# One layer of RWKV attention and a mixture of experts: the receptance product of three blocks by seven half-size products for eight, with PSUM laid out anew

## The chip, the cores and the metric

The kernel runs on one core of a Trainium2 chip. The metric is device time in microseconds (us), lower is better. Before the change it is 368.35 us, the median of four runs (367.27 to 368.84). The profile is of one further execution, recorded by the hardware profiler.

## The reference, cut to what matters

x has 2048 tokens of 512 channels in fp32. The layer norm of x feeds two branches, and both are added to x.

```python
rvk = jnp.einsum('btc,dc->btd', x, W_rvk)
r, v, k = jnp.split(rvk, 3, axis=-1)
y = jax.nn.sigmoid(r) * wkv(time_decay, time_first, k, v)
return jnp.einsum('btc,dc->btd', y, W_out)
...
biased = probs + e_score_correction_bias
_, idx = jax.lax.top_k(biased, TOP_K)
...
g = jnp.einsum('bsh,eih->bsei', x, gate_w)
u = jnp.einsum('bsh,eih->bsei', x, up_w)
act = jax.nn.silu(g) * u
expert_out = jnp.einsum('bsei,ehi->bseh', act, down_w)
out = jnp.einsum('bse,bseh->bsh', w_full[..., :n_routed], expert_out)
out = out + x * jnp.sum(w_full[..., n_routed:], axis=-1, keepdims=True)
...
x = x + _L0_attn_ref(xn, L0_attn_W_rvk, L0_attn_W_out, L0_attn_time_decay, L0_attn_time_first) + _L0_ffn_ref(xn, L0_ffn_classifier_w, L0_ffn_e_score_correction_bias, L0_ffn_gate_w, L0_ffn_up_w, L0_ffn_down_w)
```

There are 12 experts, the best two for each token, and four of the 12 only pass the token on, scaled. wkv keeps a running maximum, a numerator and a denominator for every channel, and divides at each token. r, k and v are each a product of 2048 x 512 by 512 x 512.

## The kernel before

**Tiling.** The tokens are four blocks b of TB = 512, the channels four chunks c of CC = 4 (128 partitions each). A unit is a pair (b, c): there are 16. For each unit the kernel needs k, v and r as 128 x 512 tiles, channels on partitions and tokens along the row. xnT[b] holds the transposed layer norm of a block, wrvk_sb the weights, in the order r, v, k.

**Head.** Layer norm, transposes, the router (softmax, best two, lists of tokens by expert) and the first units' products share the first 65 us. The first two units (LEAD = 2) get their products by `project` (L276), three plain products of four 512-wide matmuls each.

**Products by seven for eight.** From the third unit on, `seven` (L396) computes k and v of a unit together. Halves of the weights and halves of the tokens make two-by-two blocks, so two plain products would be eight half-size products; with sums of weights (wsum, made once) and sums of tokens (`sum_tokens`, L370, four tiles S1 to S4 per block, on DVE) it makes seven, M1 to M7. Each half-size product is two matmuls of 128 x 128 by 128 x 256 (L411). Several add up in one PSUM accumulator and are copied out between: p1 takes M1, M6, M7, M4, and p3 takes M5 and M3, and p2 M2 alone. ScalarE (ACT) copies them to k, v and a tile `more` (L436, L446, L451, L459, L470, L473); VectorE (DVE) later adds p2 to half of k and `more` to v (L421). These adds and the token sums of the next block are put on a list `owed`, which `emit_owed` hands out. r of the unit is a plain product: four 512-wide matmuls (`r_step`, L424) into a PSUM tile pr, which ACT reads with the exponential of the sigmoid (L467).

**The recurrence.** `scan` (L299) works through a unit in stages. DVE: a running maximum (L314), two subtractions (L316, L317). ACT: two exponentials (L319, L320). DVE: two scans (L326, L328) with a product by v between (L327), sums with the exponential of r (L335 to L337), a reciprocal in two halves (L340) and the product yT (L343).

**The experts.** There are 23 tiles (TILES) of 128 tokens. A tile's rows are gathered by POOL (L812), copied by ACT as 16-bit halves (`flip`, L879), transposed by a DMA on SP (L881) and put together by ACT (`unite`, L887, tile xgT). Tile 0 is transposed on PE instead (`turn`, L871, L873). The gate and up products follow (L906 into pg; two mixed tiles in L858), then tanh on ACT (L918) and two DVE operations (L919, L920), the down product (`finish`, L854 into po), a scaling on ACT (L938) and an adding indirect write by POOL (L942). `turn_act` (L928) transposes the activations of mixed tiles on PE. Weights gw and dw come by SP's queue.

**Attention rows.** `attention` (L1015) makes 128 rows of the output with four matmuls (L1043, into pw; the last row tile in two halves, L1031), DVE adds them to x's rows (L1055) or to the rows read back from the output (L1052, L1039). Eight row tiles of blocks 0 and 1 lie within the main loop. Their rows of x are read beforehand on SP (`read_xn`) and written by POOL in an adding DMA (`accumulate`, L1012), which shares POOL's queue with the gathers and the experts' writes.

**PSUM.** Four pools of two banks each (L83 to L86): ps_mm (p1, p3, some pw), ps_gu (pg, some pw and pa), ps_o (po, the other pw), ps_tr (p2, pr, px).

**The order.** Everything runs in the order in which it is written (`manual_schedule`). From about 72 us on the order comes from a table: `plan(at, generator)` enters a step at a time, and the steps are sorted by it (L1089 to L1135). Scan stages are entered every UNIT = 17.4 us (L1093), product steps in groups of four, MoE tiles evenly spread, and the attention rows at the group numbers of the dictionary `after` (L1094). Each engine executes its own instructions strictly in that order. Ahead of the table stand `fill(4)`, `emit` and `turn(0)`, which put the last products of block 0 and the first of block 1.

Of the kernel before, what the change touches and what calls it, by code (L numbers as in the profile page):

```python
# [35 lines left out]
P = 128  # L36
# [27 lines left out]
def layer(ctx: ExitStack, tc: tile.TileContext, x, w_rvk, w_out, decay, first, cls, ebias, gu, down, out):  # L64
# [11 lines left out]
    basep = pool("base", 3)  # L76
    small = pool("small", 2)
    kvp = pool("kv", 5)
    erp = pool("er", 4)
    sump = pool("sums", 1)  # L80
    five = pool("five", 2)
    dram = pool("dram", 1, space=bass.MemoryType.DRAM)
    ps_mm = pool("ps_mm", 2, space=bass.MemoryType.PSUM)  # L83
    ps_gu = pool("ps_gu", 2, space=bass.MemoryType.PSUM)
    ps_o = pool("ps_o", 2, space=bass.MemoryType.PSUM)
    ps_tr = pool("ps_tr", 2, space=bass.MemoryType.PSUM)  # L86
    routing = ExitStack()
    rp = routing.enter_context(tc.tile_pool(name="route", bufs=1))

# [209 lines left out]
    def scan(b, c):  # L299

        n = f"{b}_{c}"
        s = state[c]
        w, cf = wdec[:, c : c + 1], cfac[:, c : c + 1]
        k = kvr[b, c, "k"]
        if c == 0:
            yT[b] = xyp.tile([P, CC, TB], F32, tag="xy", name=f"yT{b}")


        obv = wk1.tile([P, 3, TB + 1], F32, tag="obv", name=f"obv{n}")
        nc.vector.tensor_copy(obv[:, :, 0:1], s[:, 0:3].unsqueeze(2))  # L310
        o, bs, bvs = (obv[:, m, 0:TB] for m in range(3))
        o2, b2, bv = (obv[:, m, 1 : TB + 1] for m in range(3))

        nc.vector.tensor_tensor_scan(o2, w.to_broadcast([P, TB]), k, s[:, 0:1], ALU.add, ALU.max)  # L314
        a2 = wk1.tile([P, TB], F32, tag="a2", name=f"a2{n}")
        nc.vector.scalar_tensor_tensor(a2, o, w, o2, ALU.add, ALU.subtract)  # L316
        nc.vector.tensor_sub(b2, k, o2)  # L317
        yield
        nc.scalar.activation(a2, a2, AF.Exp)  # L319
        nc.scalar.activation(b2, b2, AF.Exp)  # L320
        yield

        v = kvr[b, c, "v"]
        sums = wk1.tile([P, 2, TB], F32, tag="sums", name=f"sums{n}")
        sq, sp = sums[:, 0, :], sums[:, 1, :]
        nc.vector.tensor_tensor_scan(sq, bs, a2, s[:, 3:4], ALU.add, ALU.mult)  # L326
        nc.vector.tensor_mul(bv, b2, v)  # L327
        nc.vector.tensor_tensor_scan(sp, bvs, a2, s[:, 4:5], ALU.add, ALU.mult)  # L328

        er = kvr[b, c, "r"]  # L330
        den, num = sq, a2
        if b + 1 < NTB:
            nc.vector.tensor_copy(s[:, 0:3].unsqueeze(2), obv[:, :, TB : TB + 1])
            nc.vector.tensor_copy(s[:, 3:5].unsqueeze(2), sums[:, :, TB - 1 : TB])
        nc.vector.scalar_tensor_tensor(den, b2, cf, sq, ALU.mult, ALU.add)  # L335
        nc.vector.scalar_tensor_tensor(den, er, 1.0, den, ALU.add, ALU.mult)
        nc.vector.scalar_tensor_tensor(num, bv, cf, sp, ALU.mult, ALU.add)  # L337
        yield
        for hs in (slice(0, HALF), slice(HALF, TB)):
            nc.vector.reciprocal(den[:, hs], den[:, hs])  # L340
            if hs.start == 0:
                yield
        nc.vector.tensor_mul(yT[b][:, c, :], num, den)  # L343
        yield
# [17 lines left out]
    def sum_first_weights():  # L362

        wsum[1] = weights(1, 0)
        nc.vector.tensor_sub(wsum[1], weights(1, 0), weights(2, 0))

    def part(b, k, t):
        return xnT[b][:, 2 * k : 2 * k + 2, t * HALF : (t + 1) * HALF]

# [15 lines left out]
    def factors(b, n):  # L385
        return {
            1: lambda: (part(b, 0, 0), weights(2, 0)),
            2: lambda: (part(b, 1, 0), weights(2, 1)),
            3: lambda: (left[b][4], weights(1, 1)),
            4: lambda: (part(b, 1, 1), wsum[4]),  # L390
            5: lambda: (left[b][1], wsum[1]),
            6: lambda: (left[b][2], wsum[2]),
            7: lambda: (left[b][3], wsum[3]),
        }[n]()

    def seven(b, c):  # L396

# [30 lines left out]
        def next_sums(ns):  # L428
            if c == CC - 1 and b + 1 < NTB:
                for m in ns:  # L430
                    owed.append(lambda m=m: sum_tokens(b + 1, m))

        p1 = bank(ps_mm, "mm", "p1_")
        multiply(p1, 1, True, False)
# [17 lines left out]
        yield  # L452
        p2 = bank(ps_tr, "tr", "p2_")
        multiply(p2, 2, True, True)
        owed.append(lambda: add(k[:, :HALF], p2[:, :HALF]))
        next_sums((1, 2))
        yield
        multiply(p1, 7, False, False)
# [12 lines left out]
        yield  # L471
        multiply(p3, 3, False, True)
        nc.scalar.copy(more[:, :HALF], p3[:, :HALF])  # L473
        owed.append(lambda: add(v, more))
        next_sums((4,))
        yield

    def emit_owed(force=False):
        while owed and (force or not head):
            owed.pop(0)()  # L480

    head = True
    units = [(b, c) for b in range(NTB) for c in range(CC)]
# [6 lines left out]
    def all_products():  # L490
        for name, m in (("k", 2), ("v", 1), ("r", 0)):
            for u in range(LEAD):
                yield from project(*units[u], ((name, m),))
        for u in range(LEAD, len(units)):
            yield from seven(*units[u])
        emit_owed()

    products = all_products()
# [5 lines left out]

    def emit(n):
        for _ in range(n):
            owed.pop(0)()

    manual = ExitStack()
    manual.enter_context(tc.manual_schedule())  # L510
# [355 lines left out]

    def turn(i):

        pt = ps_tr.tile([P, CC, P], F32, tag="tr", name=f"px{i}")
        for c in range(CC):  # L870
            nc.tensor.transpose(pt[:, c, :], st[i]["xg"][:, c * P : (c + 1) * P], ident)  # L871
        xgT = wk1.tile([P, CC, P], F32, tag="xgT", name=f"xgT{i}")
        nc.scalar.copy(xgT, pt)  # L873
        st[i]["xgT"] = xgT
# [18 lines left out]
    def up(i, cs):  # L893

        if 0 in cs:
            st[i]["pg"] = ps_gu.tile([P, 2, INTER], F32, tag="gu", name=f"pg{i}")
        pg = st[i]["pg"]
        xgT, w = st[i]["xgT"], st[i]["w"]
        for c in cs:
# [23 lines left out]
            st[i]["actT"] = act.rearrange("p (c t) -> p c t", c=IC)  # L923

    def turn_act(i):
        pt = ps_gu.tile([P, IC, P], F32, tag="gu", name=f"pa{i}")
        for c in range(IC):
            nc.tensor.transpose(pt[:, c, :], st[i]["act"][:, c * P : (c + 1) * P], ident)  # L928
        actT = wk1.tile([P, IC, P], F32, tag="actT", name=f"actT{i}")
# [85 lines left out]
    def attention(b, js=range(NJ)):  # L1015

        for j in js:
            i = b * NJ + j
            if i < (NTB - 2) * NJ - 2 and j % 2 == 0:
                po = ps_gu.tile([P, C], F32, tag="gu", name=f"pw{i}")  # L1020
            elif i < (NTB - 2) * NJ - 2:
                po = ps_o.tile([P, C], F32, tag="o", name=f"pw{i}")
            elif j >= 2 if i in orows else j % 2 == 1:
                po = ps_mm.tile([P, C], F32, tag="mm", name=f"pw{i}")
            else:
                po = ps_o.tile([P, C], F32, tag="o", name=f"pw{i}")
            if i == NT - 1:
                for h, ph in enumerate((po, ps_tr.tile([P, C // 2], F32, tag="tr", name="pw_last"))):
                    hs = slice(h * C // 2, (h + 1) * C // 2)
                    for c in range(CC):  # L1030
                        nc.tensor.matmul(  # L1031
# [51 lines left out]
    emit(2)  # L1083
    fill(4)
    emit(1)
    head = False
    fill(4)
    turn(0)
    DONE = 11 + 9 + 16 + 2 + 12  # L1089
    STEPS = 2 * 3 * CC + 11 * (len(units) - LEAD)  # L1090


    UNIT = 17.4  # L1093
    after = {10: (0, 0), 11: (0, 1), 16: (0, 2), 17: (0, 3), 30: (1, 0), 31: (1, 1), 38: (1, 2), 39: (1, 3)}  # L1094
    groups = (STEPS - DONE) // CC + len(after)
    total = groups * 3.43 + TILES * 5.2
    table = []

# [5 lines left out]
    for u in range(1, len(units)):  # L1104
        for at in (0, 5, 7.5, 12, 14):
            plan((u - 1) * UNIT + 9 + at, stages[u])
    plan(2, flip, 1)
    plan(3, gather, 3)
    one = total / groups / CC
    for m in range(groups):  # L1110
# [97 lines left out]
```

## Time and profile before

| What | Value |
| --- | --- |
| median of four runs | 368.35 us (367.27 to 368.84) |
| profiled execution, its own time | 366.76 us |
| its span | 365.0 us |
| PE busy | 358.9 us (98%) |
| DVE busy | 298.5 us (82%) |
| ACT busy | 148.4 us (41%) |
| POOL busy | 88.8 us (24%) |
| DMA queue q1, q0 (share of 16 engines) | 55.7%, 24.7% |

The span is the time from the first to the last recorded instruction; the execution's own time also has what lies around it. PE is TensorE's matmuls, PEld its weight loads, which overlap them. A line of the page's groups names the program line, the engine, the operation, the tiles with shapes, the number, the busy time, the mean of one, and the idle time ahead of it with what ended it. A line of a list of waits reads: engine, tile and line that waited, what it waited for, then the sum in us, the number and the longest. A line of a timeline has the start, the length, the engine, the line and the operation; x4 means that four records lie in it. In a table of windows each engine has its busy time with the number of its instructions in brackets, then the granted TensorE clock, the DMA share and GB/s. The granted clock is full throughout this execution.

### The profile page before, as it was taken

To read this page: it belongs to the slowest core of one execution; us is meant where nothing else is said; L and a number is where in the kernel's file an instruction comes from. 1 tells how busy PE (TensorE), PEld (TensorE's weight loads), DVE (VectorE), ACT (ScalarE), POOL (GpSimd) and SP (SyncE) were. 2 spreads that over 40 slices of the span, in tenths; PEclk is the share of its full clock that TensorE was granted. 3 is DMA by queue.
4 is the path that set the end of the run, shared out by engine and by line. 5 is a ranking of instruction groups with operands and counts; after the bars stand their busy time and mean duration, and the time that the engine had idled before them with its cause. 6 is when DMAs were issued, how large, how long until landed. Compare 5 with 4: busy or idle time off the path is not lost. (4 is left out here: it accounts for less than half of the span.)

```text
span 365.0 us, 5058 instructions
## 1 busy us (share of the span) xinstructions
PE 358.9 (98%) x1768; PEld 240.6 (66%) x1768; DVE 298.5 (82%) x508; ACT 148.4 (41%) x267; POOL 88.8 (24%) x118
## 2 busy tenths in 40 slices
PE   8999999999999999999999999999999999999996
PEld 3555478688746676476677777787766787764444
DVE  5979989899988676999597967699969498869961
ACT  2666132344555535155433464435453526332000
POOL 6001100411222124132222222333332114212130
PEclk9999999999999999999999999999999999999999
DMA  8998931876767999969998679969799796914782
GB/s 285 403 381 323 374 117 56 331 241 201 186 186 221 317 297 301 294 107 308 326 334 208 129 207 268 271 174 287 189 271 260 220 244 121 333 23 57 175 138 93
DMA packets 47131, 84.44 MB, mean 231 GB/s; under 512 B 26496, under 2 KB 26880, under 8 KB 43328
## 3 DMA queue, kind: packets, MB, share of 16 engines
q1 hardware_dynamic: 39792, 64.05, 55.7%
q0 software_dynamic: 7312, 20.06, 24.7%
q8 instruction: 14, 0.23, 0.2%
q14 instruction: 13, 0.11, 0.1%
HBM read 63.25 MB, written 19.27 MB: 226 GB/s over the span
## 5 line engine op out<-in xcount | busy, mean ns | idle before, releaser
L906 PEld LDWEIGHTS pg<-xgT,gw 128*128 128x128 f32 x672 | 78.4, 192 | 5.9 <-issue 4.9
L906 PE MATMUL pg<-xgT,gw 128*128 128x128 f32 x672 | 78.8, 275 | 0.3 <-DMA gw<-in_gu_dram 0.3
L942 POOL DMA_INDIRECT out_dram<-yo,to_i x23 | 40.7, 1768 | 143.8 <-ACT yo L938 27.8
L340 DVE RECIPROCAL sums<-sums 128x256 f32<-128x256 f32 x32 | 54.6, 1731 | 0.0
L424 PE MATMUL pr<-xnT,wrvk 128*128 128x512 f32 x112 | 53.9, 594 | 0.0
L1043 PE MATMUL pw<-wout_sb,yT 128*128 128x512 f32 x120 | 53.7, 593 | 0.1
L1043 PEld LDWEIGHTS pw<-wout_sb,yT 128*128 128x128 f32 x120 | 22.5, 190 | 26.9 <-issue 26.8
L854 PE MATMUL po<-dw,act 128*128 128x512 f32 x84 | 39.5, 592 | 0.0
L918 ACT ACTIVATE act<-pg 128x256 f32<-128x256 f32 x23 | 8.9, 385 | 69.1 <-PE pg L906 58.9
L919 DVE SCALAR_TENSOR_TENSOR act<-act,pg 128x256 f32<-128x256 f32 x23 | 9.6, 419 | 33.4 <-ACT act L918 33.3
L812 POOL DMA_INDIRECT xg<-xs,token_i x23 | 24.8, 1079 | 45.1 <-DVE empty L763 25.2
L424 PEld LDWEIGHTS pr<-xnT,wrvk 128*128 128x128 f32 x112 | 20.4, 190 | 15.1 <-issue 13.3
L411 PE MATMUL p<-xnT,wrvk 128*128 128x256 f32 x112 | 29.1, 382 | 0.1
L411 PE MATMUL p<-S,wrvk 128*128 128x256 f32 x112 | 28.9, 380 | 0.0
L411 PE MATMUL p<-S,T 128*128 128x256 f32 x112 | 28.8, 379 | 0.0
L326 DVE TENSOR_TENSOR_SCAN sums<-obv,state,a 128x512 f32<-128x512 f32 x16 | 20.5, 1284 | 9.4 <-ACT obv L320 9.3
L411 PEld LDWEIGHTS p<-S,T 128*128 128x128 f32 x112 | 21.0, 190 | 8.7 <-issue 6.2
L854 PEld LDWEIGHTS po<-dw,act 128*128 128x128 f32 x84 | 16.0, 190 | 16.2 <-issue 14.8
L887 ACT COPY xgT<-xq 128x1024 uint16<-128x1024 uint16 x22 | 25.5, 1160 | 0.0
L411 PEld LDWEIGHTS p<-xnT,wrvk 128*128 128x128 f32 x112 | 20.8, 190 | 6.8 <-issue 2.9
L411 PEld LDWEIGHTS p<-S,wrvk 128*128 128x128 f32 x112 | 21.0, 190 | 4.4 <-issue 1.8
L879 ACT COPY xp<-xg 128x1024 uint16<-128x1024 uint16 x22 | 23.0, 1048 | 0.0
(223 smaller groups left out, 483.3 us busy)
## 6 DMA issues: line engine op xcount, KB each, us to landing
gw<-in_gu_dram SPq DMA_DIRECT2D x25, 1024.0 KB
dw<-in_down_dram SPq DMA_DIRECT2D x25, 512.0 KB
x<-in_x_dram SPq DMA_DIRECT2D x16, 256.0 KB
xs<-x SPq DMA_DIRECT2D x16, 256.0 KB
wrvk<-in_w_rvk_dram SPq DMA_DIRECT2D x3, 1024.0 KB
xrow<-xs SPq DMA_DIRECT2D x8, 256.0 KB
out_dram<-xrow POOLq DMA_DIRECT2D x8, 256.0 KB, 6.3
xrows<-xs SPq DMA_DIRECT2D x8, 256.0 KB
```

The lines of the kernel that those rows point to most:

```text
L326: nc.vector.tensor_tensor_scan(sq, bs, a2, s[:, 3:4], ALU.add, ALU.mult)
L340: nc.vector.reciprocal(den[:, hs], den[:, hs])
L411: nc.tensor.matmul(ps[:, :HALF], w[:, k, cs], a[:, k, :], start=(begin and k == 0), stop=(end and k == 1), skip_group_check=True,)
L424: nc.tensor.matmul(pr, wrvk_sb[0][:, k, cs], xnT[b][:, k, :], start=(k == 0), stop=(k == CC - 1))
L812: nc.gpsimd.indirect_dma_start(out=xg, out_offset=None, in_=xs, in_offset=bass.IndirectOffsetOnAxis(ap=token[:, column(i) : column(i) + 1] ...
L854: nc.tensor.matmul(out_, lhs[:, c, :], rhs[0][:, c, :], start=(c == 0), stop=(c == last))
L879: nc.scalar.copy(xp, st[i]["xg"].bitcast(U16).rearrange("p (c h) -> p h c", h=2))
L887: nc.scalar.copy(xgT.bitcast(U16).rearrange("p c (t h) -> p c t h", h=2), st[i]["xq"].rearrange("p (h c) t -> p c t h", h=2),)
L906: nc.tensor.matmul(pg[:, c // IC, c % IC * P : (c % IC + 1) * P], w[0][:, k, rs], xgT[:, k, :], start=(k == 0), stop=(k == CC - 1),)
L919: nc.vector.scalar_tensor_tensor(act, act, 1.0, pg[:, 0, :], ALU.add, ALU.mult)
L942: nc.gpsimd.indirect_dma_start(out=out, out_offset=bass.IndirectOffsetOnAxis(ap=index, axis=0), in_=yo[ps], in_offset=None, compute_op=ALU ...
L1043: nc.tensor.matmul(po, yT[b][:, c, j * P : (j + 1) * P], wout_sb[:, c, :], start=(c == 0), stop=(c == CC - 1),)
```

## The change

r of blocks 1 to 3 (12 units) is no longer a plain product. The seven products are now also made for r, for two chunks of channels at a time: r of chunks c and c+1 takes the places that k and v have in the other. `sevens(b, c, with_r)` makes the steps of one such set, and `pair(b, c)` runs three sets in a fixed order: A (k, v of chunk c), B (k, v of chunk c+1) and R (r of both), 21 steps of two 256-wide matmuls for a pair of units. Block 0 keeps the old way.

The weights for R's seven products come from four DVE operations (`sum_r_weights`), the first two behind `emit(1)`, the other two behind `turn(0)`. R's results are copied out of PSUM by ACT as those of k and v are, two DVE adds follow for each pair, and the exponential of r becomes an ACT operation of its own, in `scan`, between tiles in SBUF.

Behind the products of block 0 `change_banks` closes three of the PSUM pools and opens others: gu 1 bank, p2 1, p1 2, p3 1, pr 1 (both accumulators of R in its halves); ps_o keeps its 2. The eight middle attention rows all use ps_o and stand at other groups. Owed DVE work falls due two product steps after it was noted. `flip(1)` moves from the table to directly behind `turn(0)`. UNIT becomes 17.05, the pool of r tiles grows from 4 to 6, and the scratch memory for DMA descriptors is 8192 where the default is 16384.

```diff
-    erp = pool("er", 4)
+    erp = pool("er", 6)
...
+    def change_banks():
+        early.close()
+        for name, n in (("gu", 1), ("p2", 1), ("p1", 2), ("p3", 1), ("pr", 1)):
+            banks[name] = pool(f"ps_{name}", n, **psum)
...
         er = kvr[b, c, "r"]
+        if b > 0:
+            nc.scalar.activation(er, er, AF.Exp, scale=-1.0)
...
+    def sum_r_weights(first):
+        if first:
+            for n in (2, 3, 4):
+                rsum[n] = sump.tile([P, 2, 2, P], F32, tag=f"R{n}", name=f"R{n}")
+            rsum[1] = r_weights(0, 1)
+            nc.vector.tensor_sub(rsum[3], r_weights(1, 1), r_weights(0, 1))
+            nc.vector.tensor_sub(rsum[1], r_weights(0, 1), r_weights(0, 0))
+        else:
+            nc.vector.tensor_add(rsum[2], rsum[3], r_weights(0, 0))
+            nc.vector.tensor_sub(rsum[4], r_weights(1, 0), rsum[2])
...
+    def sevens(b, c, with_r):
...
+        def at(m):
+            which = {2: "p2", 3: "p3", 5: "p3"}.get(m, "p1")
+            if with_r and which != "p2":
+                ps.setdefault("pr", None)
+                if ps["pr"] is None:
+                    ps["pr"] = bank("pr", f"pr{n}")
+                h = which == "p3"
+                return ps["pr"][:, h * HALF : (h + 1) * HALF]
...
+        def m2():
+            src = multiply(2)
+            owe(lambda: nc.vector.tensor_add(t["k"][:, :HALF], t["k"][:, :HALF], src))
...
+        def m3():
+            src = multiply(3)
+            nc.scalar.copy(t["more"][:, :HALF], src)
+            owe(lambda: nc.vector.tensor_add(t["v"], t["v"], t["more"]))
...
+    def pair(b, c):
+        A, _ = sevens(b, c, False)
+        B, next_sums = sevens(b, c + 1, False)
+        R, _ = sevens(b, c, True)
+        order = "A1 A5 R1 A6 A2 R5 A7 A3 R6 A4 B1 R2 B5 B6 R7 B3 B7 R3 B2 B4 R4".split()
+        done = set()
+        for name in order:
+            while owed and owed[0][0] <= clock[0]:
+                owed.pop(0)[1]()
+            {"A": A, "B": B, "R": R}[name[0]][int(name[1])]()
...
+            clock[0] += 1
+            yield
+
+    def owe(work):
+        owed.append((clock[0] + 2, work))
...
-        for u in range(LEAD, len(units)):
+        for u in range(LEAD, CC):
             yield from seven(*units[u])
+        change_banks()
+        for b in range(1, NTB):
+            for c in range(0, CC, 2):
+                yield from pair(b, c)
...
-        pt = ps_tr.tile([P, CC, P], F32, tag="tr", name=f"px{i}")
+        pt = bank("gu", f"px{i}", (CC, P))
...
-            st[i]["pg"] = ps_gu.tile([P, 2, INTER], F32, tag="gu", name=f"pg{i}")
+            st[i]["pg"] = bank("gu", f"pg{i}", (2, INTER))
...
-        pt = ps_gu.tile([P, IC, P], F32, tag="gu", name=f"pa{i}")
+        pt = ps_o.tile([P, IC, P], F32, tag="o", name=f"pa{i}")
...
-            if i < (NTB - 2) * NJ - 2 and j % 2 == 0:
-                po = ps_gu.tile([P, C], F32, tag="gu", name=f"pw{i}")
-            elif i < (NTB - 2) * NJ - 2:
-                po = ps_o.tile([P, C], F32, tag="o", name=f"pw{i}")
-            elif j >= 2 if i in orows else j % 2 == 1:
-                po = ps_mm.tile([P, C], F32, tag="mm", name=f"pw{i}")
+            if i >= (NTB - 2) * NJ - 2 and (j >= 2 if i in orows else j % 2 == 1):
+                po = bank("p1", f"pw{i}")
             else:
                 po = ps_o.tile([P, C], F32, tag="o", name=f"pw{i}")
...
     emit(1)
+    sum_r_weights(True)
     head = False
     fill(4)
     turn(0)
+    flip(1)
+    sum_r_weights(False)
...
-    UNIT = 17.4
-    after = {10: (0, 0), 11: (0, 1), 16: (0, 2), 17: (0, 3), 30: (1, 0), 31: (1, 1), 38: (1, 2), 39: (1, 3)}
+    UNIT = 17.05
+    after = {10: (0, 0), 12: (0, 1), 16: (0, 2), 18: (0, 3), 28: (1, 0), 30: (1, 1), 37: (1, 2), 38: (1, 3)}
...
-    plan(2, flip, 1)
...
-    nc = bacc.Bacc("TRN2", target_bir_lowering=False, num_devices=1)
+    nc = bacc.Bacc("TRN2", target_bir_lowering=False, num_devices=1, dynamic_dma_scratch_size=8192)
```

## The prediction, made before the changed kernel ran

> **What bounds the kernel now.** I read the page first, for the share of each engine, then what PE waited for, then the chain of waits, and then timelines of the places that the change touches. All times are us of the one profiled execution: its span is 365.0 and its own time 366.76, so 1.76 lie around the span. Part 1 of the page:
>
> ```profile
> PE 358.9 (98%) x1768; PEld 240.6 (66%) x1768; DVE 298.5 (82%) x508; ACT 148.4 (41%) x267; POOL 88.8 (24%) x118
> ```
>
> What PE waited for, with the sum, the number and the longest wait:
>
> ```profile
> PE warm L513 <- DVE ones L136: 1.1, 1, 1.1
> PE pt L244 <- ACT x L233: 0.5, 2, 0.3
> PE pt L244 <- DVE x L231: 0.5, 1, 0.5
> PE pg L906 <- DMA gw<-in_gu_dram: 0.3, 1, 0.3
> ```
>
> The chain that ended last, whose last pieces are:
>
> ```profile
> 344.94 13.11 PE pw L1043 x30
> 358.06 1.73 PE pw L1031 x8
> 359.78 1.74 PE pw_last L1031 x8
> 361.52 0.02 issue
> 361.55 0.42 DVE orows L1039
> ```
>
> PE is busy nearly from end to end, its four waits sum to 2.4, and it carries the end. So a matmul taken from PE is worth its full time as long as PE finds its operands ready afterwards. The granted clock is full in all 40 slices of part 2, so rows of one stage hold in another. DVE (82%) is the next engine, and how it stands is read by stage. The table of windows (PE, PEld, DVE, ACT, POOL busy in 143 to 175) and DVE's list of waits say:
>
> ```profile
> 143.00:175.00 32.00, 31.74 (x162) 18.69 (x161) 29.81 (x42) 14.13 (x24) 10.11 (x8) 1.00 0.94 258
> ```
>
> ```profile
> DVE act L919 <- ACT act L918: 33.3, 14, 4.7
> DVE sums L326 <- ACT obv L320: 9.3, 9, 2.0
> ```
>
> In that stage DVE is busy 29.81 of 32, but over the run it waits 33.3 for MoE activations, up to 4.7 at once. It is a second bound in places, with pauses in which it catches up.
>
> **What the change takes from PE.** One timeline, the start of block 1, gives the prices (start, duration, engine, line, operation):
>
> ```profile
> 66.76 1.03 PE L411 MATMUL p<-S,wrvk 128*128 128x256 f32 x4
> 67.62 1.03 PE L411 MATMUL p<-xnT,wrvk 128*128 128x256 f32 x4
> 68.26 0.68 DVE L377 TENSOR_TENSOR S<-xnT 128x512 f32<-128x512 f32 x1
> 68.48 1.88 PE L424 MATMUL pr<-xnT,wrvk 128*128 128x512 f32 x4
> ...
> 70.20 1.03 PE L411 MATMUL p<-S,T 128*128 128x256 f32 x4
> ...
> 72.85 0.62 ACT L320 ACTIVATE obv<-obv 128x512 f32<-128x512 f32 x1
> ...
> 73.50 1.28 DVE L326 TENSOR_TENSOR_SCAN sums<-obv,state,a 128x512 f32<-128x512 f32 x1 [2.02 <-ACT obv L320]
> 73.62 1.06 ACT L879 COPY xp<-xg 128x1024 uint16<-128x1024 uint16 x1
> ```
>
> Durations of matmuls overlap, so I count from start to start. Each fp32 matmul makes two records. The four narrow records from 67.62 to 68.48 are one product of two 256-wide matmuls: 0.86. The four wide records from 68.48 to 70.20 are two 512-wide matmuls: 1.72. Two units' r took eight wide matmuls, 8 x 0.86 = 6.88; as seven products they take 7 x 0.86 = 6.02. That saves 0.86 a pair. The finer row starts, 429 ns a wide record and 215.5 a narrow one, make it 16 x 0.429 - 28 x 0.2155 = 0.83, and for six pairs **-5.0**.
>
> The Trainium skill, "TensorE: Matmul & The Clock Gate", part "Back-to-back issue gap", speaks against this: in streams of weight loads and matmuls it gives about 81 ns at 128 columns and 131 at 512, so a narrower matmul costs more per column. Put between these, about 98 at 256 columns is my estimate, and 28 narrow records would cost 2.7 where 16 wide ones cost 2.1, some 0.6 a pair slower, +3.9 in all. The trace does not agree: 215.5 is half of 429 within 0.3%.
>
> One small stall goes too: in the old order M4 of a unit and M1 of the next follow at once in the buffers of one pool, and once (115.87) PE started 0.25 late there. In the new order every use of an accumulator stands at least two steps (1.72) behind the one before: **-0.25**. The wait of 0.3 for gw (0.42 from start to start) I leave as it is.
>
> **What it adds on DVE and ACT.** DVE gets, per pair, one 256-wide add (0.41, as L421 of k) and one 512-wide add (0.68, as L421 of v): 6 x 1.09 = 6.5, and once four weight sums of 0.69: 2.8; 9.3 in all, under the 33.3 + 9.3 of its waits. ACT gets per pair six 256-wide copies (0.37, as L446) and two exps from SBUF (0.63, as L319) for two from PSUM (0.60, L467): 2.3, 14 over the run, on an engine busy 41%. Neither is a cost by itself; what counts is where an instruction that waits holds up others behind it.
>
> Head of block 1 (67 to 110). The pair begins A1 A5, while the old unit began M1, r, r, M6, M5. A5 needs the first token sum S1, which DVE ends at 68.26 + 0.68 = 68.94 and which nothing in the change makes earlier; A5 would start at 68.48. Stall **+0.5**. Flip(1) now stands directly behind turn(0): its ACT copy (1.06, L879) and its transposing DMA on SP go ahead of scan (1,0)'s two exps. The DMA comes earlier and holds up nothing I can find on SP; the copy puts the scan from 73.50 to about 75.0. The weight sums (until about 74.2 on DVE) hide in that wait, which was 2.0 before. From here DVE is 1.5 late; the v add, now ahead of the second reciprocal, and the r adds make it 2.2 late at unit (1,1) and 3.4 at unit (1,2). DVE itself keeps nobody waiting, but the exps of a scan (L319, L320) wait for DVE's subtraction, and behind them on ACT stand the copies that free PSUM and the copy xgT (L887) that the next gate products need. At unit (1,1) the exps ended at 87.5 before; 2.2 later, with the activation (0.39) and the copy of B6's product (0.37), gives 90.5, some 0.4 to 0.5 after B7 wants its accumulator: **+0.45**. At unit (1,2) xgT of tile 3 ended at 103.99, 1.79 before its products; 3.4 of lateness leaves **+1.5**, PE standing about where it stood (0.8 gained, 0.95 lost). Head together +2.45, by the rows between 0.5 (all but the first covered) and 4.
>
> Middle. The idle stretches of DVE (4.2 at 117.5, 3.1 at 140.7, 4.0 at 174) return the lateness. The PSUM tiles that became single are covered: between the last write of one use and the first of the next, PE has, by the listing of the changed kernel at these prices, at least 5.2 of other work for gu, 8.8 for p2, 4.4 for ps_o, against an ACT or DVE release that took about 1.4 behind PE for a gate tile, up to 2.7. The moved attention rows issue their xrow reads on SP and their adding writes on POOL at other groups; POOL's gather of tile 15 had some 2.4 of margin and keeps about that. The smaller DMA scratch I cost at nothing, since few descriptors are in flight at a time. **+0.3**, between 0 and 3: the upper end is one lateness like 3.4 in 143 to 175, where DVE had only 2.2 free and gets 1.1 more.
>
> R's two accumulators lie in one bank; R5 waits for ACT's copy of R1. The copy starts 0.41 behind the product and takes 0.37, ended 0.78 after it, while the next R step comes two steps (1.72) later: nothing, if ACT is free. The Trainium skill, "PSUM — Partial Sum Buffer", section on bank collisions, says to guard PSUM by bank and quadrant, not by address; by it this wait is due although the halves do not overlap, and it is counted in the slower rival below.
>
> Tail. The last rows of attention wait for DVE's last scan, which ended at 347.05 against PE's 347.5. That chain gets one v add shorter but starts behind the later r add and behind a PE that ends its MoE tile sooner; by the rows DVE is done 25.4 to 25.9 behind the last gate tile, PE ready at 25.3: **+0.2**, at most 0.8.
>
> **Sum.** -5.0 - 0.25 + 2.45 + 0.3 + 0.2 = -2.3: a span of 362.7 and 364.5 for the profiled kind of execution. The profiled time of before lies 1.6 under the median of its four runs (368.35), so I subtract from the median: 368.35 - 2.3 = 366.05, said as **366.1**. A measurement of this kernel can tell about 0.3%, 1.1.
>
> **Rivals.**
> *The full gain.* DVE and ACT have pauses enough, and the lateness of the head never reaches PE, apart from S1. For it: PE's list names no wait for DVE or ACT behind 45 us. Against: the copies behind exps on ACT had 0.7 to 1.8 to spare, and my lateness is more. -5.25 + 0.5 = -4.75: 363.6. Chance 0.24.
> *The gain is eaten, no change.* The same waits as in my sum, but the head at its upper 4 and the middle at 1: -5.25 + 4 + 1 + 0.3 = 0: 368.4. Chance 0.12.
> *Slower: ACT's queue hands DVE's lateness to PE.* It decides at a lateness of some 2 at a scan's first exps: then the copies behind them come after PE wants the bank pr, p1 or the tile xgT. Each such unit costs the lateness less the slack, 3.4 - 1.8 = 1.6 as at unit (1,2). If DVE does not recover (it has 1.1 more to do per pair, and 2.2 free in 143 to 175), five of the eleven later units at 1.6 make 8: -5.25 + 8 = +2.8: 371. For it: 29.81 of 32. Against: the 33.3 that DVE waited, mostly where a gate tile sets the pace, and that a stalled PE gives DVE time. Chance 0.14, with 0.02 of it for narrow matmuls dearer than the trace has them.
> That the change does not do what it says is excluded for PE's part: the listing of the changed kernel has 84 narrow r matmuls where 48 wide ones were.
> The forecast itself has 0.50. So faster by over 0.3%: 0.50 + 0.24 = 0.74, less 0.02 for its own upper edge: 0.72; within 0.3%: 0.13; slower: 0.15. The range goes from the full gain with the first stall hidden too (363.1) to a third of the slower rival's surplus: 369.3.
>
> **What would show it.** The r products at 215 to 216 ns a record and PE busy near 354; a wait of p3 for S1 of about 0.5 near 68.5; a wait of PE at pg of tile 3 near 106, or of p1 near 90, released by ACT; DVE's wait for L320 at its scan near 75; no PE wait for ACT or DVE between 120 and 320. Wrong it would be if PE's list shows no wait in the head (then about 363.6), or waits for ACT in most units (then 368 and more).

## The result, and the profile after

The changed kernel takes 366.30 us (median of 52 runs), the kernel before 367.45 (78 runs, now that there are more). The ratio is 0.9969, 95% interval 0.9958 to 0.9980: 1.15 us faster, where 2.3 were forecast. The forecast of 366.1 lies only 0.2 from the measured time, and that is in part luck: it was counted down from 368.35, the median of the first four runs of the kernel before, which is 0.90 above the median of all 78. Some executions of these kernels show a mean granted clock of 0.995 or less and take some 2 us longer than the others (four of the six of e8 below, whose other two took 362.29 and 362.78), so that where medians are close the gaps in the traces decide. The profiled execution of the changed kernel has a span of 363.8 for 365.0, and a time of its own of 365.62 for 366.76. Part 1 of the page of the changed kernel:

```profile
PE 354.9 (98%) x1840; PEld 254.0 (70%) x1840; DVE 306.1 (84%) x524; ACT 157.8 (43%) x303; POOL 89.5 (25%) x118
```

PE is busy for 4.0 less, DVE for 7.6 more and ACT for 9.4 more. (The prediction's 5.0 on PE is counted from start to start, and its 9.3 on DVE and 14 on ACT are sums of durations, while in the profile neighbouring instructions overlap a little, as the exponentials and copies from 88.61 on below do.) What PE waited for in the changed kernel:

```profile
PE pg L1011 <- ACT xgT L1040: 1.2, 1, 1.2
PE warm L666 <- DVE ones L148: 1.1, 1, 1.1
PE pt L256 <- DVE x L243: 0.6, 1, 0.6
PE pt L256 <- ACT x L245: 0.5, 2, 0.3
PE p L555 <- DVE S L408: 0.4, 1, 0.4
PE pw L1192 <- DVE xrows L1204: 0.4, 1, 0.4
PE p L555 <- ACT v L578: 0.3, 1, 0.3
PE pg L1059 <- DMA gw<-in_gu_dram: 0.3, 1, 0.3
PE pw L1192 <- DVE xrow L1204: 0.3, 1, 0.3
```

Before, nothing on this list came from DVE or ACT after the head. Now there are five such waits, and each can be dated. I call a **gap** what lies between the starts of two neighbouring matmul records beyond the spacing of their form (112 ns at 128 columns, 215.5 at 256, 429 at 512); a gap is somewhat more than the wait in the list. A gap is named by a time shortly before it begins: the record that comes late starts about the gap and another 0.4 to 0.7 later (A5 at 69.25, tile 3 at 107.56). Gaps of over 0.15 behind 45 us, in us:

| place | before | changed | released by |
| --- | --- | --- | --- |
| 68.2, A5 | - | 0.60 | DVE's token sum S1 |
| 89.5, B7 | - | 0.50 | ACT's copy of B6's product |
| 105.7, gate products of expert tile 3 | - | 1.39 | ACT's copy xgT |
| 115.9, M1 behind M4 | 0.25 | - | |
| gw of an expert tile | 0.42 at 173 | 0.47 at 118.5 | DMA |
| 194.5, attention row tile 3 | - | 0.44 | DVE's addition of row tile 2 |
| 250.8, gate products of tile 16 | - | 0.22 | ACT's copy xgT |
| 343, the If | 0.31 | 0.31 | |
| 345.1, row tile 12 | - | 0.52 | DVE's addition of row tile 8 |

All excess over the spacings behind 45 us sums to 2.3 before and 6.0 in the changed kernel: +3.6 against the 5.0 taken from PE, or -1.4. The spans differ by 1.2; the rest lies in the first 45 us. The two largest places, on ACT (start, duration, engine, line, operation):

```profile
84.45 0.38 ACT L583 COPY more<-p 128x256 f32<-128x256 f32 x1
88.61 0.63 ACT L331 ACTIVATE a<-a 128x512 f32<-128x512 f32 x1 [3.78 <-DVE a L328]
89.21 0.63 ACT L332 ACTIVATE obv<-obv 128x512 f32<-128x512 f32 x1
89.75 0.36 ACT L1071 ACTIVATE act<-pg 128x256 f32<-128x256 f32 x1
90.01 0.36 ACT L578 COPY v<-p 128x256 f32<-128x256 f32 x1
...
102.93 0.37 ACT L574 COPY r<-pr 128x256 f32<-128x256 f32 x1 [0.49 <-PE pr L555]
105.23 0.63 ACT L331 ACTIVATE a<-a 128x512 f32<-128x512 f32 x1 [1.93 <-DVE a L328]
105.83 0.63 ACT L332 ACTIVATE obv<-obv 128x512 f32<-128x512 f32 x1
106.37 1.14 ACT L1040 COPY xgT<-xq 128x1024 uint16<-128x1024 uint16 x1
```

ACT sat idle for 3.78 and for 1.93 in front of an exponential that waited for DVE, with copies queued behind it that TensorE needed: the copy of B6's product could have run at about 88.4, 1.06 behind the start of that product (87.33) as in the kernel before, and xgT at 103.30, when ACT came free.

The chain that ended last, followed back from the end, is PE for the last 20 us in the kernel before and breaks off there. In the changed kernel it goes on, and its shares of the span are:

```profile
PE 53%; DVE 22%; DMA 4%; ACT 3%; issue 2%; SPq 1%; DVEq 0%; ACTq 0%
```

DVE is on the path for a fifth of the span, while PE is as busy as before in per cent. Since the chain of before breaks off, the two cannot be set side by side; but in e11 below, where the gaps of the loop are gone, it reads PE 86%, DVE 8%. So a few short waits were enough to lead that much of the chain over DVE.

One correction of names: where the prediction and the expectations speak of the scans of units (1,0), (1,1) and (1,2) near 74, 89 and 105 us, these are the scans of (0,0), (0,1) and (0,2), which run while the products of block 1 are made.

### The profile page after: what moved, and what is told of

It is laid out like the page before. It is cut to its first block, busy times and chain, and to the rows that moved or that the text cites. A ratio compares the mean times of both kernels' runs of the same rounds, so it can differ in the third digit from the quotient of the medians.

```text
span 363.8 us, 5277 instructions
## 1 busy us (share of the span) xinstructions
PE 354.9 (98%) x1840; PEld 254.0 (70%) x1840; DVE 306.1 (84%) x524; ACT 157.8 (43%) x303; POOL 89.5 (25%) x118
## 4 chain that ended last, share of the span: by engine, by line
PE 53%; DVE 22%; DMA 4%; ACT 3%; issue 2%; SPq 1%; DVEq 0%; ACTq 0%
PE pg L1059 16%; PE p L555 13%; PE pw L1192 8%; PE po L1007 6%; PE pr L555 6%; DVE sums L354 5%; DMA gw<-in_gu_dram 4%; DVE obv L326 2%; DVE sums L340 1%; DVE sums L338 1%; DVE yT L357 1%; PE po L1011 1%; DVE tok L878 1%; PE pg L1011 1%; DVE sums L350 1%
## 5 line engine op out<-in xcount | busy, mean ns | idle before, releaser
L1095 POOL DMA_INDIRECT out_dram<-yo,to_i x23 | 42.3, 1838 | 140.2 <-DMA out_dram<-yo,to_i 25.7
L1192 PE MATMUL pw<-wout_sb,yT 128*128 128x512 f32 x120 | 54.5, 595 | 0.8 <-DVE xrows L1204 0.4
L338 DVE TENSOR_TENSOR_SCAN sums<-obv,state,a 128x512 f32<-128x512 f32 x16 | 20.5, 1282 | 7.1 <-ACT obv L332 6.8
L555 PE MATMUL p<-S,T 128*128 128x256 f32 x96 | 25.0, 382 | 0.3 <-ACT v L578 0.3
L555 PE MATMUL p<-S,wrvk 128*128 128x256 f32 x96 | 24.7, 380 | 0.4 <-DVE S L408 0.4
L555 PE MATMUL p<-xnT,wrvk 128*128 128x256 f32 x96 | 24.7, 379 | 0.0
L555 PEld LDWEIGHTS p<-S,T 128*128 128x128 f32 x96 | 17.9, 190 | 6.8 <-issue 2.4
L340 DVE TENSOR_TENSOR_SCAN sums<-obv,state,a 128x512 f32<-128x512 f32 x16 | 20.6, 1284 | 0.6
L555 PEld LDWEIGHTS p<-S,wrvk 128*128 128x128 f32 x96 | 17.7, 190 | 4.2 <-issue 1.2
L326 DVE TENSOR_TENSOR_SCAN obv<-wdec,state,k 128x512 f32<-128x512 f32 x16 | 20.5, 1279 | 0.0
L555 PEld LDWEIGHTS p<-xnT,wrvk 128*128 128x128 f32 x96 | 17.8, 190 | 3.4 <-issue 1.2
```

The source lines that it names most:

```text
L555: nc.tensor.matmul(dst, rows_(k), a[:, k, :], start=(first and k == 0), stop=(k == 1), skip_group_check=True,)
L1095: nc.gpsimd.indirect_dma_start(out=out, out_offset=bass.IndirectOffsetOnAxis(ap=index, axis=0), in_=yo[ps], in_offset=None, compute_op=ALU ...
L1192: nc.tensor.matmul(po, yT[b][:, c, j * P : (j + 1) * P], wout_sb[:, c, :], start=(c == 0), stop=(c == CC - 1),)
```

## The experiments

My theory: PE saves its full 5.0, and the separate gaps give 3.6 of it back, each through an engine that executes in order and stands in front of a wait for DVE. The rivals: the narrow products save less than 5.0; DVE is a bound all along; the gaps share one slack, so that mending one moves it to the next.

### e1: the first reader of S1 one step later

```diff
+        if (b, c) == (1, 0):
+            order[1:3] = "R1", "A5"
```

> The changed kernel with one swap in the first pair alone: A1 R1 A5 for A1 A5 R1, so that the first step that reads the token sum S1 comes one step (0.86 us) later. The trace of the changed kernel shows TensorE 0.60 us late at that place (A5 behind DVE's S1, L408). Theory A (S1's end on DVE, 69.1, is the cause, and what TensorE loses there is lost for good): that gap disappears, and the time falls by 0.6 us, from 0.9969 of the kernel before to about 0.9953. Rival B (the gap is paid anyway, because DVE and ACT set the pace of the head, and the two later gaps at 89.5 and 105.7 us follow DVE, not TensorE): the gap disappears, the two later gaps grow by as much together, and the time stays (0.9969). I hold B for likelier: the chain DVE subtraction, exponential, copy of the tile for the gate products does not depend on S1's reader.

Measured: 365.33, ratio 0.9939 (0.9910 to 0.9967); the span is 363.0 for 363.8. The gap at 68.2 is gone, those at 89 and 105 are 0.50 and 1.39 as they were, only 0.7 earlier. **A holds, and B, which I had held for likelier, falls.** The reason shows on ACT in this run:

```profile
71.94 0.59 ACT L1028 COPY xgT<-px 128x512 f32<-128x512 f32 x1
72.42 1.05 ACT L1034 COPY xp<-xg 128x1024 uint16<-128x1024 uint16 x1
73.37 0.63 ACT L331 ACTIVATE a<-a 128x512 f32<-128x512 f32 x1
```

The exponential starts at 73.37, in the changed kernel at 74.06. DVE's scan starts from it and the one after it; on ACT both stand behind the copy of px (line L1028 here), and px comes from PE, behind A5. So what PE lost at A5, DVE lost as well. (The verdict rests on the gaps and the spans; the interval of the times reaches to within 0.0002 of B's value.)

### e2: flip(1) where it was

```diff
     turn(0)
-    flip(1)
...
+    plan(2, flip, 1)
     plan(3, gather, 3)
```

> The changed kernel with flip(1) back in the table at 2, that is behind the two exponentials of unit (1,0)'s predecessor scan on ACT, as in the kernel before. In the changed kernel its copy (1.05 us) stands ahead of these exponentials, and DVE's scan at 75.24 waited 0.95 us for them. Theory A (this order is one source of the lateness that the gaps at 89.5 (0.50) and 105.7 us (1.39) show): the scan starts at about 74.3, all that follows on DVE comes 0.95 earlier, the gap at 89.5 is gone and that at 105.7 becomes about 0.9; time 0.95 us less, 0.9943 of the kernel before. Rival B (the added DVE operations alone make the lateness, the flip is hidden): both gaps stay, no change (0.9969). Rival C: the flip's transposing DMA, now later, makes TensorE wait for the tile at 83.7 us, and the time grows.

Measured: 365.20, 0.9938 (0.9909 to 0.9967), span 362.9. The gap at 89.5 is gone, the one at 105.7 is 0.79 for 1.39 (forecast about 0.9), and a new one of 0.26 stands at 83.0, at the gate products of tile 1, whose tile is now late (C, in small); the wait for gw near 118 is 0.71 for 0.47. A holds: the early flip was a source of the lateness, and it was worth only 0.26 to tile 1.

### e3: no additions of r on DVE

```diff
-            owe(lambda: nc.vector.tensor_add(t["v"], t["v"], t["more"]))
+            if not with_r:
+                owe(lambda: nc.vector.tensor_add(t["v"], t["v"], t["more"]))
```

(and the same for the 256-wide addition)

> The changed kernel without the twelve DVE adds of r (256 and 512 wide, one of each for every pair); r of blocks 1 to 3 therefore lacks one of its seven products in one half and the sum of two in the other, everything else is computed. DVE has 6.5 us less to do. Theory A (DVE's lateness reaches TensorE only through ACT's queue in a few places): ahead of the exponentials of the scan at 105.2 stand 0.41 and 0.69 us of these adds, so the gap at 105.7 falls from 1.39 to about 0.3, the tail gap at 345.1 (0.52) shrinks to about 0, the gap at 68.2 (0.60) and that at 89.5 (0.50) stay; 1.4 to 1.9 us less in all, 0.992 to 0.993 of the kernel before. Rival B (DVE is a bound all along the loop): 4 us or more less, 0.986. Rival C (DVE's adds are hidden): no change, 0.9969.

Measured: 364.44, 0.9912 (0.9879 to 0.9945). The gap at 105.7 is 0.45, that at 250.8 is gone, those at 68, 89 and 194 stay. Taking 6.5 us from DVE saves 1.2 by the spans (362.6 for 363.8) and 2.1 by the ratios, not 4: **DVE is no bound all along (B falls), nor are its additions free (C falls)**. One part of A fails: the tail gap is 0.51, as before. It does not hang on these additions.

### e4: two moves in ACT's order

```diff
+    EARLY = {3: 30.9}
...
-        if i + 1 < n:
+        if i + 1 < n and i + 1 not in EARLY:
             unite(i + 1)
...
+            if (u, at) == (1, 5):
+                at = 5.65
             plan((u - 1) * UNIT + 9 + at, stages[u])
+    for i, at in EARLY.items():
+        plan(at, unite, i)
```

> The changed kernel with two moves in ACT's order and nothing else: the exponentials of unit (1,1)'s scan stand behind the activation of tile 1 and the copy of B6's product (instead of ahead of both), and the copy that makes the tile for the gate products of expert tile 3 stands ahead of the exponentials of the next scan. Theory A (the two gaps at 89.5 and 105.7 us, 0.50 and 1.39, come from ACT waiting for DVE with ready copies queued behind it): both gaps disappear, DVE is not slower by it, and 1.9 us are saved: 0.9917 of the kernel before. Rival B (ACT or DVE is simply late by then, whatever the order): the gaps move to the next place where TensorE needs DVE's or ACT's result, and 0.5 us or less are saved (0.9955 and above).

Measured: 363.68, 0.9900 (0.9849 to 0.9950). Both gaps are gone, no new one came, and the excess behind 45 us is 1.9 less. What PE waited for, past the head:

```profile
PE p L555 <- DVE S L408: 0.4, 1, 0.4
PE pw L1194 <- DVE xrows L1206: 0.4, 1, 0.4
PE pw L1194 <- DVE xrow L1206: 0.3, 1, 0.3
PE pg L1059 <- DMA gw<-in_gu_dram: 0.3, 1, 0.3
```

DVE's subtraction ahead of the exponentials at 89 came no earlier than in the changed kernel (18.57 behind the start of A5 in both runs: 69.25 to 87.82, and here 71.35 to 89.92); the copies only no longer stood behind it. A holds.

### c1 and e5: the control, and r as a plain product in the new layout

> The changed kernel itself once more, beside the others on the same chip. Expected as before: 0.9969 of the kernel before, gaps of TensorE at 68.2, 89.5, 105.7, 194.5, 250.8 and 345.1 us.

Measured: 366.10, 0.9964 (0.9943 to 0.9986), span 364.1, with the same gaps at the same places (excess behind 45 us 5.8).

```diff
-        if b > 0:
-            nc.scalar.activation(er, er, AF.Exp, scale=-1.0)
...
-        R, _ = sevens(b, c, True)
...
+                nc.tensor.matmul(
+                    wide["ps"],
+                    wrvk_sb[0][:, k, u * P : (u + 1) * P],
+                    xnT[b][:, k, :],
...
+                    nc.scalar.activation(kvr[b, u, "r"], wide["ps"], AF.Exp, scale=-1.0)
...
+        last = r_of(c + 1, 3), r_of(c + 1, 2)
+        R = dict(zip((1, 5, 6, 2, 7, 3), [r_of(c, k) for k in range(CC)] + [r_of(c + 1, k) for k in range(2)]))
+        R[4] = lambda: [work() for work in reversed(last)]
...
-    sum_r_weights(True)
...
-    sum_r_weights(False)
```

(r of chunk c stands in the steps R1, R5, R6 and R2, r of chunk c + 1 in R7, R3 and twice in R4.)

> The changed kernel with r of blocks 1 to 3 as a plain product again: the eight 512-wide matmuls of a pair stand in the seven places of R's steps, each r whole in the bank pr and read by ACT with the exponential straight from PSUM; R's weight sums and adds are gone. The order of everything else, the PSUM layout, flip(1), the attention rows and UNIT are those of the changed kernel. TensorE has 5.0 us more to do, DVE 9.3 less. Theory A (the seven products are worth their full 5.0 on TensorE, the adds cost 1.4 of it at 105.7 and 250.8, and the new layout and order cost about 2 by themselves): some 3.5 us more than the changed kernel, 1.005 to 1.008 of the kernel before, with the gaps at 68.2 and 194.5 still there, that at 105.7 about 0.3. Rival B (narrow products are worth less than 5.0, and the changed kernel's small gain is mainly that): at most 1.5 us more than the changed kernel, 1.001 or below. Rival C (new layout and order cost nothing): 1.000.

Measured: 368.15, 1.0014 (0.9993 to 1.0036), 2.05 above the control where I expected 3.5. What PE waited for in this kernel, past the head:

```profile
PE p L553 <- ACT k L572: 0.5, 1, 0.5
PE p L553 <- ACT v L576: 0.4, 1, 0.4
PE pw L1211 <- DVE xrows L1223: 0.4, 1, 0.4
```

The first line is A5 again (gap 0.62): ACT's copy of k and DVE's S1 ended 0.15 apart there, and A5 started 0.15 behind S1's end (69.33 and 69.48), as in the changed kernel (69.11 and 69.25). The second is B7 (0.57) and the third the tail (0.57).

The excess behind 45 us is 3.3 here, 2.3 before and 5.8 in the control. So the layout, the order and the flip cost 1.0 by themselves (A said about 2, C nothing; the interval of the times alone would allow no change), and the seven products for r bring 2.5 of gaps with their 5.0: 5.0 - 2.5 = 2.5, and the spans of the two differ by 2.3 (366.4 and 364.1). Rival B read the small distance of the times as narrow products being worth less. Its bound of 1.5 is passed, and the traces say no as well: the work is 5.0 less, and the distance is small because the gaps at 105.7, 118, 194 and 250 are not there with r as a plain product. They do not all hang on r's additions: e3, without these, still has 0.45 at 105.7, 0.35 at 118 and 0.44 at 194. What I had mis-sized is that 2.5, which I put at 1.4; that the gap at 194.5 would stay here and 105.7 keep 0.3 was wrong too. On the other hand the gaps at 68, at 89 and in the tail are here without the seven products for r: they belong to the new layout, order and flip.

### e8, e7 and e11: mending all gaps, and the tail

e8 is e1 and e4 together, with tile 16 in EARLY at 167.3, and:

```diff
-            plan(CC * (m + 1) * one + 1, group)
+            plan(CC * (m + 1) * one + (0.8 if m == 16 else 1), group)
...
+            if i in (NT - 4, NT - 3):
+                po = bank("gu" if i == NT - 4 else "p2", f"pw{i}")
-            if i >= (NTB - 2) * NJ - 2 and (j >= 2 if i in orows else j % 2 == 1):
+            elif i >= (NTB - 2) * NJ - 2 and (j >= 2 if i in orows else j % 2 == 1):
```

> The changed kernel with every gap that its trace shows mended by a move in the order: A1 R1 A5 in the first pair (0.60 at 68.2); the exponentials of unit (1,1) behind the copy of B6's product (0.50 at 89.5); the tile copies of expert tiles 3 and 16 ahead of the exponentials beside them (1.39 at 105.7, 0.32 at 250.8); the DVE addition of attention row tile 2 two tenths earlier in the table, ahead of the next scan's first operations (0.54 at 194.5); the attention row tiles 12 and 13 in the banks gu and p2, which nobody uses by then, for those of ps_o (0.52 at 345.1). Theory A (these gaps are separate, each one a wait in an engine's queue, and nothing else holds TensorE): they add up, 3.8 us less than the changed kernel, 0.986 to 0.988 of the kernel before. Rival B (they share one slack, of DVE): with the first two mended the rest moves elsewhere, and about 2 are saved (0.991). For the tail apart: if the gap at 345 stays with the new banks, it is DVE's last yT and not the bank.

Measured: 364.41, 0.9887 (0.9856 to 0.9919). Every gap of the loop of over 0.15 is gone, that of gw too, but the gap of the tail is 1.30. In this profiled execution TensorE's granted clock was 0.81 between 9 and 18 us, so its span (363.2) says nothing; its gaps do. The wait, and the instructions around it:

```profile
PE pw L1198 <- DVEq L1307: 1.1, 1, 1.1
```

```profile
343.50 0.69 DVE L357 TENSOR_TENSOR yT<-a,sums 128x512 f32<-128x512 f32 x1
344.11 1.40 DVE L1210 SCALAR_TENSOR_TENSOR xrows<-xrows,zw,pw 128x512 f32<-128x512 f32 x2
345.14 3.49 POOL L1169 DMA_DIRECT2D out_dram<-xrows  x4 [7.22 <-DVE xrows L1210]
345.71 3.67 PE L1198 MATMUL pw<-wout_sb,yT 128*128 128x512 f32 x8 [1.13 <-DVEq L1307]
```

Row tile 12 now waits for no addition, but for DVE's queue at the If (L1307), which DVE reaches behind both additions. Two runs tell that apart from mere lateness. The first, e7, has the two bank lines of e8's edit and nothing else:

> The changed kernel with attention row tiles 12 and 13 in the banks gu and p2 for those of ps_o, and nothing else. In the run with all gaps mended the gap near 345 did not go but grew to 1.30, put down to DVE's queue at the If (line 1297 in the changed kernel). Theory A (a PE instruction behind the If that needs a result DVE wrote ahead of it, here the last yT, starts only when DVE has passed the If, that is after both additions of rows 8 and 9; in the old bank the first of them released it 0.7 sooner): the gap grows from 0.52 to about 1.2. Rival B (it grew there only because TensorE had gained time on DVE): it is at most 0.5 here.

Measured (one execution, 366.49): with this edit alone the gap at 345 is 1.23 for 0.52, again released by DVE's queue at the If. So B falls, and the new banks were the wrong cure. The reason that A gives is not shown, though. In e7 row tile 12 started with DVE's first operation behind the If:

```profile
347.22 1.96 PE L1194 MATMUL pw<-wout_sb,yT 128*128 128x512 f32 x4 [1.07 <-DVEq L1299]
347.23 1.41 DVE L1206 SCALAR_TENSOR_TENSOR xrows<-xrows,zw,pw 128x512 f32<-128x512 f32 x2 [0.21 <-DVEq L1299]
```

In the changed kernel the same row tile, behind the same If, needs a result that DVE wrote ahead of the If as well, the addition of row tile 8, and it started 0.7 before DVE's first operation behind the If:

```profile
346.34 6.25 PE L1192 MATMUL pw<-wout_sb,yT 128*128 128x512 f32 x14 [0.35 <-DVE xrows L1204]
347.06 1.41 DVE L1204 SCALAR_TENSOR_TENSOR xrows<-xrows,zw,pw 128x512 f32<-128x512 f32 x2 [0.21 <-DVEq L1297]
```

So a result from ahead of the If does not by itself wait for the If. Why the new banks put the wait there stays open.

The second, e11, is e8 without the two bank lines:

> The run with all gaps mended, but with attention row tiles 12 and 13 in the banks of the changed kernel again. Theory A of the tail (the new banks made it wait for both of DVE's additions): the gap near 345 falls from 1.30 to about 0.6, and the time is 0.7 below that run. Rival B (TensorE only waits for DVE's chain, whatever the bank): the gap stays at 1.3 and the time as well. Against the kernel before I expect 0.987.

Measured: **362.44, 0.9865 (0.9838 to 0.9891)**, the fastest kernel here, 3.7 below the control. Its waits of PE, complete:

```profile
PE warm L668 <- DVE ones L148: 1.1, 1, 1.1
PE pt L256 <- DVE x L243: 1.1, 1, 1.1
PE pt L256 <- ACT x L245: 0.5, 2, 0.3
PE pw L1196 <- DVE xrows L1208: 0.4, 1, 0.4
```

The tail gap is 0.52 again although PE has gained its time on DVE, so it was the banks that made it 1.30. (The times do not show that 0.7: 362.44 here, beside the 362.29 and 362.78 of e8 named with the result.) The excess behind 45 us is 2.3, as in the kernel before: the 5.0 of PE's work is now all gain (367.1 - 362.4 = 4.7). The gaps were separate, and rival "one slack" falls.

### e12: more work behind the last products

```diff
-    after = {10: (0, 0), 12: (0, 1), 16: (0, 2), 18: (0, 3), 28: (1, 0), 30: (1, 1), 37: (1, 2), 38: (1, 3)}
+    after = {10: (0, 0), 12: (0, 1), 16: (0, 2), 18: (0, 3), 28: (1, 0), 36: (1, 1), 37: (1, 2), 38: (1, 3)}
```

(on top of e11)

> The kernel of e11_no_tail_edit with attention row tile 5 (block 1, second) at group 36 instead of 30, behind the last products. TensorE then has 3.44 us more work between the last product and the If, and DVE's last scan, which follows these products, starts 3.44 earlier against it; DVE gets one addition of 0.74 more in that stretch. Theory A (the tail gap is DVE's last scan, 25 us long without a pause, against the work that TensorE has left): the gap near 345 goes, 0.5 us less than e11. Rival B (the scan before it already keeps DVE busy, so that an earlier product starts nothing earlier): the gap grows by the addition's 0.7. Rival C: the two banks of ps_o make row 5 wait for DVE's addition, a new gap ahead of 340.

Measured: 371.59, 1.0106 (1.0066 to 1.0146). Rival C, and dearer than I thought: two waits of about 3 us, the first ending at 323.97, the second at 352.46.

```profile
PE po L1009 <- DVE xrow L1208: 3.2, 1, 3.2
PE pw L1196 <- DVE xrows L1208: 3.0, 1, 3.0
```

```profile
319.86 1.28 DVE L340 TENSOR_TENSOR_SCAN sums<-obv,state,a 128x512 f32<-128x512 f32 x1
...
323.17 0.74 DVE L1208 SCALAR_TENSOR_TENSOR xrow<-xrow,zw,pw 128x512 f32<-128x512 f32 x1
```

The addition that frees row 5's bank for the next down product stands behind a scan on DVE. The tail's 0.5 stays open: no run removed it, and A could not be read here behind C's waits.

Whether the smaller scratch for DMA descriptors costs anything was not tried apart: with the default size the larger tiles of the changed kernel do not fit into SBUF (one pool of 17.0 KB per partition, 15.1 left). No wait in the traces points to it.

## Why the prediction was right, point by point

- **PE, -5.0: right.** The listing has the 84 narrow matmuls for 48 wide ones, their records stand 215.5 apart, and e5 against the control gives 2.3 + 2.5 = 4.8 by spans and gaps. (215.5 is half of 429 within 0.5%, not the 0.3% of the prediction.) The figures of the Trainium skill, "TensorE: Matmul & The Clock Gate", section "Back-to-back issue gap", by which narrow matmuls would be dearer for each column, are not borne out by these fp32 products.
- **The 0.25 of M4 and M1: right**, it is gone. The wait for gw was neither gained nor lost, it moved from 173 to 118.5.
- **Head, +2.45: right, term by term.** A5 0.60 for 0.5, B7 0.50 for 0.45, tile 3 1.39 for 1.5; together 2.49. The named cause of each was tested: S1 (e1), the flip and the additions (e2, e3), ACT's order (e4). What I had wrong afterwards, in e1's expectation, is that DVE's chain is independent of PE there: it starts from px.
- **Middle, +0.3: the first mis-sized term, some 0.8.** All excess between 120 and 320 rose by some 0.8, apart from gw, and the sign "no PE wait for ACT or DVE between 120 and 320" failed. Row tile 3 waits 0.44 at 194.5, since DVE's addition of row tile 2 is entered at 111.44 (the table's own time), just behind a scan's first operations at 111.30, and tile 16's products 0.22 at 250.8 for xgT, again behind a pair of exponentials; each has another 0.1 beside it. Moving these two entries took both gaps away (e8, e11). Each is a near tie in the table that the working looked for only in the head. The cover of the single PSUM banks held: neither p2 nor pr shows a wait, and p3 only that for S1. R's two accumulators share the bank pr, which the Trainium skill ("PSUM — Partial Sum Buffer", section "PSUM bank collisions raise a hardware error") says to guard by bank and quadrant, not by address; no wait of PE for pr is in the list. The worry about 143 to 175 was unfounded: DVE was busy for 27.2 of 32 there, PE for all.
- **Tail, +0.2: the second mis-sized term, 0.52.** The working put it down to the later addition of r, as e3's expectation did, and that was wrong: without r's additions the gap is 0.51 (e3), with r as a plain product 0.57 (e5). The wait is for DVE's addition of row tile 8, which DVE makes behind the last yT; it comes with the new layout and order, and which part of these brings it stays open.
- The sum was -2.3. With the measured terms it is -5.0 - 0.25 + 2.5 + 0.8 + 0.5, some -1.4, and -1.2 by the profiled spans. The forecast's sign, its mechanism and its largest terms were right; its size was double, by the middle and the tail. That the time itself came so near is luck in the part named with the result: the base was 0.90 too high.
- The rivals: the full gain did not come by itself, but e11 shows that it was there to be had. The slower one, lateness handed on by ACT's queue, is the mechanism of three gaps here (89.5, 105.7, 250.8), in three units rather than five or more.

## What to carry to other kernels

When work is moved from the bound engine to one that has slack on average, look at each in-order queue for an instruction that waits for the second engine, and at what stands behind it that the first needs: ACT stood idle for 1.9 us with a ready copy behind an exponential, and two moves by a hair in the table (e4, 1.9 us of gaps) were worth more than the whole change (1.15). Price these places singly, all along the loop and not only where the change starts: near ties in a timetable are where they arise. And a step that ends a wait by a new buffer helps only if the buffer was the last thing to come; here, at an If, it lengthened the wait by 0.7.

## What the runs showed of the hardware that I had not expected

In the tail, a matmul behind the If was released by DVE's passing of the If when it had a bank of its own, and started 0.7 us later than with the bank that DVE's first addition freed (gaps 1.23 and 0.52). Whether that is the chip's doing or comes from how the program's waits are laid at the If, no run here tells.

In e12 the 3.2 us pause was followed by a spell of TensorE at half rate. In the table of windows the granted clock is the column behind POOL's:

```profile
319.00:324.00 5.00, 1.80 (x8) 0.86 (x6) 4.85 (x8) 0.00 (x0) 0.00 (x0) 1.00 0.00 0
324.00:329.00 5.00, 5.00 (x8) 2.17 (x9) 4.96 (x5) 0.69 (x1) 1.57 (x1) 0.66 0.00 0
329.00:334.00 5.00, 5.00 (x13) 2.16 (x12) 2.28 (x4) 2.25 (x4) 1.19 (x3) 1.00 0.39 52
```

The clock fell to 0.66 in the 5 us behind the pause and was full again after; four records there stood 0.42 too far apart each, so the pause cost some 1.7 us beyond itself. Four late records follow the second wait, of 3.0, too. How long a pause must be for that, these runs do not say. The gap of 1.39 at 105.7 left the changed kernel's clock at 1.00; but in e8's profiled execution the clock fell in the head, where TensorE had paused for no more than 1.31 since its first matmuls (the wait for x, which ended at 9.93):

```profile
9.00:18.00 9.00, 7.80 (x39) 4.58 (x40) 7.78 (x24) 5.84 (x10) 0.00 (x0) 0.81 1.06 399
```

With 1.06 at the same place e11's clock stayed at 1.00. That the pause of 1.31 brought the fall is not shown.
